# One operand of the first layer's vector instructions moved to PSUM in a two-layer graph kernel

## The chip, the cores and the metric

The kernel runs on one core of one Trainium2 chip. The metric is the device time of one execution in microseconds, the median over the runs of a kernel. Lower is better. The engines are called by the profile's names: PE (TensorE), DVE (VectorE), ACT (ScalarE), POOL (GpSimd) and SP (SyncE).

## The reference

Two message-passing layers run over 6250 nodes of 128 features and 200000 edges sorted by destination `dst`. Each layer normalises the nodes, applies a ReLU, sends messages along the edges and adds the sum per destination to the nodes. The first layer, the one that is changed, is an attention layer with 8 heads:

```python
z = (feat @ W).reshape(N, HEADS, PER_HEAD)
el = jnp.einsum('nhp,hp->nh', z, attn_l)
er = jnp.einsum('nhp,hp->nh', z, attn_r)
e = jax.nn.leaky_relu(el[src] + er[dst], negative_slope=NEG_SLOPE)
emax = jax.ops.segment_max(e, dst, num_segments=N)
a = jnp.exp(e - emax[dst])
denom = jax.ops.segment_sum(a, dst, num_segments=N)
agg = jax.ops.segment_sum(z[src] * a[:, :, None], dst, num_segments=N)
out = agg / jnp.maximum(denom, 1e-09)[:, :, None] + bias
```

The second layer gathers `h[src]` again, multiplies it with edge attributes and with the outputs of a small network over 8 edge features, and sums by `dst`. It is not changed.

## The kernel before

The edges lie in 1563 tiles of 128, one edge on each partition. Sixteen tiles make a block, so there are 98 blocks. A first stage computes a row of 136 numbers for every node (128 of `z`, 8 of `el`) and writes it to a table in HBM; `er` stays on the chip.

The first layer then works block by block, one pass of a loop over `g` for each:

- **Gathers.** `take_rows` fetches the table rows of a block's source nodes, one indirect DMA for each tile, issued by POOL at line L832 (`gather`) three blocks ahead. The index column `src_col` (the profile's `fsrc`) lies in SBUF. The destination tiles come from a pool of five. In 31 blocks one of the sixteen tiles comes row by row on SP's queue instead (L1067), so POOL issues 1516 gathers in this loop, after 16 for the first block.
- **One-hot matrices.** `one_hot` (L1086) compares a row 0 to 127 (`iota`) with the position of each edge's destination in its window. It makes four tiles per DVE instruction, four instructions per block, called through `ends_of`. PE turns them (`turned`, L1132), ACT copies them out (L1134), and PE multiplies them with `er` in three bf16 parts (`er_of`, L1143); `er_sum` (L1149) adds the parts.
- **Logits and maxima.** `logits` adds `el` and `er` (L1156), applies the leaky ReLU (L1157) and turns the result on PE into a PSUM bank `pe` (L1160). `maxima` runs two segmented scans along the edges, forward (L1166) and backward (L1168). `neighbours` moves the edge values of the maxima between tiles and blocks with four small matmuls (L1175 to L1184), and ACT copies the two columns out (L1187).
- **Weights and sums.** `weights`, one block later, joins the neighbours' maxima with the block's own (L1193, L1195), subtracts (L1198) and takes the exponential. `weighted` (L1210) scales the rows, and `sums` (L1215) adds them per destination on PE.
- **Nodes.** In every second block a tile of 128 nodes is finished (`node_x` to `node_out`): lines L1225 to L1238 on DVE, then a transpose into a PSUM bank `p_n` (L1259), a ReLU on ACT (L1261), a matmul into the same bank (L1266) and a copy out (L1268), which is written to the second layer's table.

The order of the work on PE, DVE, ACT and SP is written out by hand as the order of these calls. A semaphore wait therefore holds everything behind it on its engine. POOL has only gathers to issue. After the loop the last three groups of tiles are written out one by one. The second layer's gathers start when the last rows of its table have been written. In that layer `iota` already lies in PSUM (tile `held`, the profile's `p_i`), and so does one factor of the messages.

Of the kernel before, what the change touches and what calls it, by code (L numbers as in the profile page):

```python
# [18 lines left out]
P = 128  # L19
H = 8  # L20
# [9 lines left out]
KB = 16  # L30
# [933 lines left out]
def even_edges(tc, v):  # L964
    nc = tc.nc
    NX, TU, TG, NB, KT, MC = (v[k] for k in (
        "NX", "TU", "TG", "NB", "KT", "MC"))
    t0, t1, ident, eps, er3, z_first, dstt, nums = (v[k] for k in (
        "t0", "t1", "ident", "eps", "er3", "z_first", "dstt", "nums"))
    xp, dstc, y4, f8, bias, out, moments, deviation, normal, gather, tiles_of = (v[k] for k in (  # L970
        "xp", "dstc", "y4", "f8", "bias", "out", "moments", "deviation", "normal", "gather", "tiles_of"))
    with ExitStack() as ctx:
# [6 lines left out]
        iota = const.tile([P, P], F32, name="fiota")  # L979
# [29 lines left out]
        shift = const.tile([P, 3, P], F32, name="fshift")  # L1009
# [35 lines left out]
        with tc.tile_pool(name="fat_ps", bufs=1, space=PSUM) as at_ps:  # L1045
            col = const.tile([P, P], F32, name="fcol")
            n = NB - 1
# [35 lines left out]
        def one_hot(t, m, iota=iota):  # L1083

            s = s_pool.tile([P, 4, P], F32, name="s")
            nc.vector.tensor_tensor(s[:, :m], iota[:, None, :].to_broadcast([P, m, P]),  # L1086
                                    dloc[:, t : t + m].unsqueeze(2).to_broadcast([P, m, P]),
                                    OP.is_equal)
            return s
# [17 lines left out]
        with tc.manual_schedule(engines=in_order), \  # L1107
# [2 lines left out]
                tc.tile_pool(name="l0_ps", bufs=1, space=PSUM) as l0_ps:  # L1110


            def ends_of(c, q):

                if 4 * q < c["kt"] and q == len(c.setdefault("s", [])):
                    c["s"].append(one_hot(c["b"] * KB + c["o"] + 4 * q, min(4, c["kt"] - 4 * q)))

            def masks_of(c):
                o, kr = c["o"], c["kt"] * H
# [23 lines left out]
                        nc.tensor.matmul(c["p_er"][:, 4 * q + k].rearrange("p s h -> p (s h)"),  # L1143
                                         c["d", q][:, k, :], er_w, start=True, stop=True)

            def er_sum(c):
                kt = c["kt"]
                er = c["er"] = l0.tile([P, KB, H], F32, name="er")
                nc.vector.tensor_reduce(er[:, :kt], c["p_er"][:, :kt].rearrange("p t s h -> p t h s"),  # L1149
                                        AX.X, OP.add)  # L1150

            def logits(c, bank="pe"):
                kt = c["kt"]
                kr = kt * H
                e_s = l0.tile([P, KB, H], F32, name="e_s")
                nc.vector.tensor_add(e_s[:, :kt], c["z"][:, :kt, F:], c["er"][:, :kt])  # L1156
                nc.vector.scalar_tensor_tensor(e_s[:, :kt], e_s[:, :kt], 0.2, e_s[:, :kt],  # L1157
                                               op0=OP.mult, op1=OP.max)
                pe = c["pe"] = l0_ps.tile([P, 512], F32, name=bank, bufs=2 if bank == "pe" else 1)
                nc.tensor.transpose(pe[:kr, :P], e_s[:, :kt].rearrange("p t h -> p (t h)"), ident)  # L1160

            def maxima(c):

                kr, mk, pe = c["kt"] * H, c["mk"], c["pe"]
                mx = c["mx"] = l0.tile([P, 2, P], F32, name="mx", bufs=4)
                nc.vector.tensor_tensor_scan(mx[:kr, 0, :], mk[:kr, :P], pe[:kr, :P], 0.0,  # L1166
                                             OP.add, OP.max)
                nc.vector.tensor_tensor_scan(mx[:kr, 1, ::-1], mk[:kr, P:0:-1], mx[:kr, 0, ::-1], 0.0,  # L1168
                                             OP.add, OP.max)

            def neighbours(c, before, after):

                kr, pe, mx = c["kt"] * H, c["pe"], c["mx"]
                up, dn = pe[:kr, 2 * P : 2 * P + 1], pe[:kr, 2 * P + 1 : 2 * P + 2]
                nc.tensor.matmul(dn, shift[:kr, 2, :kr], mx[:kr, 1, P - 1 :], start=True,  # L1175
                                 stop=before is None)
                if before is not None:
                    kb = before["kt"] * H
                    nc.tensor.matmul(dn, shift_to[kb][:kb, :kr], before["mx"][:kb, 1, P - 1 :],
                                     start=False, stop=True)  # L1180
                nc.tensor.matmul(up, shift[:kr, 0, :kr], mx[:kr, 1, 0:1], start=True, stop=after is None)
                if after is not None:
                    ka = after["kt"] * H
                    nc.tensor.matmul(up, shift[:ka, 1, P - kr :], after["mx"][:ka, 1, 0:1],  # L1184
                                     start=False, stop=True)
                ud = c["ud"] = l0.tile([P, 2], F32, name="ud")
                nc.scalar.copy(ud[:kr], pe[:kr, 2 * P : 2 * P + 2])  # L1187

            def weights(c):

                kr, pe, mx, mk, ud = c["kt"] * H, c["pe"], c["mx"], c["mk"], c["ud"]
                m1 = l0.tile([P, P], F32, name="m1")
                nc.vector.scalar_tensor_tensor(m1[:kr], mk[:kr, P + 1 : 2 * P + 1], ud[:kr, 0:1],  # L1193
                                               mx[:kr, 1, :], op0=OP.add, op1=OP.max)
                nc.vector.scalar_tensor_tensor(m1[:kr], mk[:kr, 2 * P + 1 :], ud[:kr, 1:2],  # L1195
                                               m1[:kr], op0=OP.add, op1=OP.max)
                a = l0.tile([P, P], F32, name="a")
                nc.vector.tensor_sub(a[:kr], pe[:kr, :P], m1[:kr])  # L1198
                nc.scalar.activation(a[:kr], a[:kr], AF.Exp)
                nc.tensor.transpose(pe[:, P : P + kr], a[:kr], ident[:kr, :kr])  # L1200
                nc.scalar.copy(c["z"][:, : c["kt"], F:],  # L1201
                               pe[:, P : P + kr].rearrange("p (t h) -> p t h", h=H))
# [50 lines left out]

            def node_t(u):
                n = u["n"]
                p_n = l0_ps.tile([P, 512], F32, name="p_n")
                p_n = u["p_n"] = p_n.rearrange("p (j f) -> p j f", f=P)
                for j in range(n):
                    nc.tensor.transpose(p_n[:, j, :], u["xn"][:, j, :], ident)  # L1259
                h_t = u["h_t"] = l0n.tile([P, 2, P], F32, name="h_t")  # L1260
                nc.scalar.activation(h_t[:, :n], p_n[:, :n], AF.Relu)  # L1261

            def node_s(u):
                i, n, p_n = u["i"], u["n"], u["p_n"]
# [17 lines left out]
            shift_to = {}  # L1282
# [6 lines left out]
            NG = len(cs)  # L1289
# [51 lines left out]
            for g in range(NG - 3):  # L1341
                take_rows(g + 3)
                filled(0, g, cs[g]["z"], ZW)
                rows_until(rows, g + 0.5)
                for n in late:
                    node_out(n)
                if g % 2 == 0 and g // 2 + 2 < NX - 2:
                    node_rows(g // 2 + 2, 1)
                rows_until(rows, g + 1)
                c, b4 = cs[g], (cs[g - 1] if g else None)  # L1350
                n1 = cs[g + 1] if g + 1 < NG else none
                n2 = cs[g + 2] if g + 2 < NG else none
# [12 lines left out]
                turned(n1, 1)  # L1365
                er_of(n1, 0)
                if b4:
                    weights(b4)
                for n in nodes:
                    node_x(n)  # L1370
                er_of(n1, 1)
                turned(n1, 2)
                if b4:
                    bank_of(b4)
                    weighted(b4, 0)
                turned(n1, 3)
                er_of(n1, 2)
                if b4:
                    weighted(b4, 8)
                for n in nodes:  # L1380
                    node_d(n)
                    node_h(n)
                ends_of(n2, 2)
                er_of(n1, 3)
                if b4:
                    sums(b4, 0)
                for n in nodes:
                    node_t(n)
                if n1 is not none:
                    er_sum(n1)  # L1390
                ends_of(n2, 3)
                for n in nodes:
                    node_s(n)
                late = nodes
                if b4:
                    sums(b4, 8)
                if g == NG - 4:
                    for q in range(4):
                        ends_of(c1, q)
                    masks_of(c1)  # L1400
                    for q in range(4):
                        turned(c1, q)
                        er_of(c1, q)
                    er_sum(c1)
            node_rows(NX - 2, 2)
            for n in late:
                node_out(n)
# [373 lines left out]
```

## Time and profile before

| What | Value |
|---|---|
| Median of three runs | 6103.52 us (6102.03 to 6114.51) |
| Profiled execution, its own time | 3960.89 us |
| Its span, first to last instruction | 3959.1 us |
| POOL busy, share of the span | 2955.5 us, 75% |
| PE busy, share of the span | 2823.8 us, 71% |
| DVE busy, share of the span | 2189.6 us, 55% |
| ACT busy, share of the span | 1390.4 us, 35% |

The profile is of one execution, and its own time lies 2142.6 us under the median of the runs. Times inside it add up to its own span, not to the median. In the profile the first layer's loop takes the stretch from about 70 to 2000 us, the second layer that from about 2030 us to the end. In a row of the costliest groups the two numbers after the first bar are busy microseconds and mean nanoseconds of one instruction; after the second bar stands the idle time of the engine just before them and what ended it. "Issue" means that nothing the profile shows was waited for.

### The profile page before, as it was taken

How to read it: one execution, taken by the hardware profiler on the slowest of the kernel's cores; microseconds unless marked ns; L12 is line 12 of the kernel's file. 1: busy time of each engine (PE TensorE's matmuls, PEld its weight loads, DVE VectorE, ACT ScalarE, POOL GpSimd, SP SyncE). 2: the span in 40 equal slices, each digit the busy share in tenths (PEclk: the TensorE clock that was granted, in tenths of full speed). 3: DMA queues.
4: the chain of work that ended last, by engine and by line, in shares of the span. 5: the costliest groups of instructions: out<-in, count | busy, mean ns of one | idle time of the engine just before them, and what ended most of it. 6: DMA issues, size and time to landing. Idle time of an engine off the chain costs nothing. (4 is left out here: it accounts for less than half of the span.)

```text
span 3959.1 us, 62173 instructions
## 1 busy us (share of the span) xinstructions
PE 2823.8 (71%) x14593; PEld 2368.9 (60%) x14593; DVE 2189.6 (55%) x5379; ACT 1390.4 (35%) x3512; POOL 2955.5 (75%) x3096
## 2 busy tenths in 40 slices
PE   3666666666666666666676888788788787788777
PEld 3655555555665666565555666566566566666565
DVE  5444444444444444444455776666666666666666
ACT  3322222223222323222233444444444444344443
POOL 6777777777777777777757777777777777777776
PEclk6666666666666666666678999999999999999999
DMA  6222222222222222222212222222222222222221
GB/s 176 58 60 61 60 61 61 60 59 61 60 61 59 59 61 60 61 59 60 59 45 60 62 62 62 62 63 62 61 63 62 61 61 61 62 61 62 61 62 49
DMA packets 188124, 249.35 MB, mean 63 GB/s; under 512 B 77888, under 2 KB 137952, under 8 KB 187744
## 3 DMA queue, kind: packets, MB, share of 16 engines
q0 software_dynamic: 98048, 207.27, 22.2%
q1 hardware_dynamic: 89408, 37.92, 3.7%
q8 instruction: 118, 1.93, 0.2%
q14 instruction: 262, 2.15, 0.2%
q10 hardware_dynamic: 288, 0.07, 0.0%
HBM read 234.73 MB, written 9.99 MB: 62 GB/s over the span
## 5 line engine op out<-in xcount | busy, mean ns | idle before, releaser
L832 POOL DMA_INDIRECT g<-ft,fsrc x3048 | 2921.8, 959 | 957.7 <-issue 873.5
L1544 PE MATMUL p_u<-mj,s 128*128 128x256 f32 x3126 | 794.3, 398 | 263.7 <-DVE mj L1536 261.9
L1544 PEld LDWEIGHTS p_u<-mj,s 128*128 128x128 f32 x3126 | 585.5, 195 | 442.0 <-DVE mj L1536 369.3
L1215 PE MATMUL p_u<-g,s 128*128 128x136 f32 x3062 | 578.9, 368 | 0.5 <-DVE g L1210 0.5
L1215 PEld LDWEIGHTS p_u<-g,s 128*128 128x128 f32 x3062 | 554.2, 272 | 0.6 <-DVE g L1210 0.6
L1511 ACT ACTIVATE p_w<-p_w,yb 128x64 f32<-128x64 f32 x1563 | 450.3, 288 | 119.5 <-PE p_w L1507 79.6
L1527 DVE TENSOR_TENSOR vy<-g,p_i 128x384 f32<-128x384 f32 x391 | 215.6, 551 | 462.4 <-DMA g<-ft,fsrc 374.6
L1156 DVE TENSOR_TENSOR e_s<-g,er 128x128 f32<-128x128 f32 (+1 forms) x98 | 28.4, 290 | 735.0 <-DMA g<-ft,fsrc 697.0
L1507 PE MATMUL p_w<-fa3p,h 128*128 128x256 f32 x1564 | 409.7, 385 | 0.0
L1132 PE MATMUL p_d<-fident,s 128*128 128x128 f32 x1563 | 390.5, 416 | 5.2 <-DVE s L1086 5.2
L1507 PEld LDWEIGHTS p_w<-fa3p,h 128*128 128x128 f32 x1564 | 288.7, 195 | 118.7 <-issue 52.1
L1160 PE MATMUL pe<-fident,e_s 128*128 128x128 f32 x98 | 39.8, 406 | 444.6 <-DVE e_s L1157 444.6
L1125 ACT COPY mk<-p_m 128x385 f32<-128x385 f32 (+1 forms) x99 | 47.7, 481 | 875.1 <-PE p_m L1122 875.1
L1132 PEld LDWEIGHTS p_d<-fident,s 128*128 128x128 f32 x1563 | 316.9, 228 | 44.2 <-DVE s L1086 32.1
L1492 ACT ACTIVATE h<-p_h,fb 128x512 f32<-128x512 f32 x196 | 134.7, 687 | 568.8 <-PE p_h L1490 567.5
L1134 ACT CAST d<-p_d 128x512 bf16<-128x512 f32 x391 | 228.9, 586 | 198.5 <-PE p_d L1132 149.9
L1210 DVE TENSOR_TENSOR g<-g,pe 128x1024 f32<-128x1024 f32 x193 | 225.4, 1209 | 127.3 <-ACT g L1201 121.8
L1160 PEld LDWEIGHTS pe<-fident,e_s 128*128 128x128 f32 x98 | 16.7, 170 | 461.2 <-issue 452.5
L1086 DVE TENSOR_TENSOR s<-p_i,fdloc 128x512 f32<-128x512 f32 x391 | 266.0, 680 | 14.5 <-ACT p_i L1486 14.5
L1086 DVE TENSOR_TENSOR s<-fiota,fdloc 128x512 f32<-128x512 f32 x391 | 265.8, 681 | 5.9 <-ACT fmasks L1036 5.8
L1490 PE MATMUL p_h<-ft,fa1p 128*128 128x128 f32 x1568 | 217.7, 284 | 62.5 <-DMA ft<-in_e_f_dram 62.4
L1490 PEld LDWEIGHTS p_h<-ft,fa1p 128*128 128x128 f32 x1568 | 214.2, 200 | 79.3 <-issue 63.7
(177 smaller groups left out, 3363.2 us busy)
## 6 DMA issues: line engine op xcount, KB each, us to landing
r<-ft SPq DMA_DIRECT2D x3968, 0.5 KB
r<-ft SPq DMA_DIRECT2D x3968, 0.5 KB
g<-ft,fsrc POOLq DMA_INDIRECT x3048
ft<-in_e_f_dram SPq DMA_DIRECT2D x98, 64.0 KB
yb<-in_e_y_dram SPq DMA_DIRECT2D x98, 32.0 KB
fx_all<-in_e_xp_dram SPq DMA_DIRECT2D x48, 64.0 KB
ft<-sv SPq DMA_DIRECT2D x47, 64.0 KB
out_dram<-fx_all SPq DMA_DIRECT2D x47, 64.0 KB
```

What stands on the lines that cost most here:

```text
L832: nc.gpsimd.indirect_dma_start(out=to[:, k, :width], out_offset=None, in_=table, in_offset=bass.IndirectOffsetOnAxis(ap=src_col[:, t : t + ...
L1086: nc.vector.tensor_tensor(s[:, :m], iota[:, None, :].to_broadcast([P, m, P]), dloc[:, t : t + m].unsqueeze(2).to_broadcast([P, m, P]), OP. ...
L1132: nc.tensor.transpose(p_d[:, k, :], c["s"][q][:, k, :], ident)
L1134: nc.scalar.copy(d[:, :m], p_d[:, :m])
L1210: nc.vector.tensor_mul(zh, zh, p_a[:, k0 : k0 + m].unsqueeze(3).to_broadcast([P, m, H, D]))
L1215: nc.tensor.matmul(c["p_u"][:, :ZW], c["s"][k // 4][:, k % 4, :], c["z"][:, k, :], start=c["o"] + k == 0, stop=c["o"] + k == KT[c["b"]] - 1)
L1490: nc.tensor.matmul(p_h[:, q, :], a1p[:, q0 + q, :], c["ft"], start=True, stop=True)
L1492: nc.scalar.activation(c["h1"], p_h, AF.Silu, bias=b1)
L1507: nc.tensor.matmul(w[:, k : k + n].rearrange("p k a u -> p (k a u)"), c["h2"][q // 4][:, q % 4, :], a3p[:, :n].rearrange("p k f -> p (k f) ...
L1511: nc.scalar.activation(w[:, k, ::2, :], w[:, k, ::2, :], AF.Copy, scale=c["yb"][:, k0 + k, 0:1])
L1527: nc.vector.tensor_mul(vy, v_n, y_p)
L1544: nc.tensor.matmul(blk[b]["p_u"][:, :MW], u["s"][:, k, :], u["mj"][:, k, :], start=k0 + k == 0, stop=k0 + k == KT[b] - 1)
```

## The change

`iota`, `er`, both scans' results and the joined maxima are put into PSUM. A bank `p_n`, until now taken anew for each tile of nodes, becomes one permanent tile that holds the node work, `er` (columns 128 to 255) and `iota` (columns 384 to 511). The scans write into free columns of the block's own bank `pe`. [...]ACT copies the first and last column of the backward scan to a small SBUF tile `mx`. Two calls of `er_sum` at the end of the loop keep an SBUF tile (`aside`).

```diff
+            p_n = l0_ps.tile([P, 512], F32, name="p_n")
+            er_p, iota_p = p_n[:, P : 2 * P].rearrange("p (t h) -> p t h", h=H), p_n[:, 3 * P :]
+            nc.scalar.copy(iota_p, iota)
...
-                    c["s"].append(one_hot(c["b"] * KB + c["o"] + 4 * q, min(4, c["kt"] - 4 * q)))
+                    c["s"].append(one_hot(c["b"] * KB + c["o"] + 4 * q, min(4, c["kt"] - 4 * q), iota_p))
...
-            def er_sum(c):
+            def er_sum(c, aside=False):
-                er = c["er"] = l0.tile([P, KB, H], F32, name="er")
+                er = c["er"] = l0.tile([P, KB, H], F32, name="er") if aside else er_p
...
+                pe = c["pe"] = p_n if bank == "p_n" else l0_ps.tile([P, 512], F32, name=bank, bufs=2)
...
-                mx = c["mx"] = l0.tile([P, 2, P], F32, name="mx", bufs=4)
-                nc.vector.tensor_tensor_scan(mx[:kr, 0, :], mk[:kr, :P], pe[:kr, :P], 0.0,
+                m0, m1 = pe[:kr, P : 2 * P], pe[:kr, 3 * P :]
+                nc.vector.tensor_tensor_scan(m0, mk[:kr, :P], pe[:kr, :P], 0.0, OP.add, OP.max)
+                nc.vector.tensor_tensor_scan(m1[:, ::-1], mk[:kr, P:0:-1], m0[:, ::-1], 0.0,
                                              OP.add, OP.max)
-                nc.vector.tensor_tensor_scan(mx[:kr, 1, ::-1], mk[:kr, P:0:-1], mx[:kr, 0, ::-1], 0.0,
-                                             OP.add, OP.max)
+                mx = c["mx"] = l0.tile([P, 2], F32, name="mx", bufs=4)
+                nc.scalar.copy(mx[:kr], m1[:, :: P - 1])
...
-                nc.vector.scalar_tensor_tensor(m1[:kr], mk[:kr, P + 1 : 2 * P + 1], ud[:kr, 0:1],
-                                               mx[:kr, 1, :], op0=OP.add, op1=OP.max)
-                nc.vector.scalar_tensor_tensor(m1[:kr], mk[:kr, 2 * P + 1 :], ud[:kr, 1:2],
-                                               m1[:kr], op0=OP.add, op1=OP.max)
+                m1, m2 = pe[:kr, 3 * P :], pe[:kr, P : 2 * P]
+                nc.vector.scalar_tensor_tensor(m2, mk[:kr, P + 1 : 2 * P + 1], ud[:kr, 0:1],
+                                               m1, op0=OP.add, op1=OP.max)
                 a = l0.tile([P, P], F32, name="a")
-                nc.vector.tensor_sub(a[:kr], pe[:kr, :P], m1[:kr])
+                nc.vector.scalar_tensor_tensor(a[:kr], mk[:kr, 2 * P + 1 :], ud[:kr, 1:2],
+                                               m2, op0=OP.add, op1=OP.max)
+                nc.vector.tensor_sub(a[:kr], pe[:kr, :P], a[:kr])
...
             def node_t(u):
-                p_n = l0_ps.tile([P, 512], F32, name="p_n")
-                p_n = u["p_n"] = p_n.rearrange("p (j f) -> p j f", f=P)
+                u["p_n"] = p_n.rearrange("p (j f) -> p j f", f=P)
...
-                    er_sum(n1)
+                    er_sum(n1, g == NG - 4)
...
-                    er_sum(c1)
+                    er_sum(c1, True)
```

More of the change, by code (lines that the diff above doesn't have):

```diff
@@ L1158, in logits @@
                                                op0=OP.mult, op1=OP.max)
-                pe = c["pe"] = l0_ps.tile([P, 512], F32, name=bank, bufs=2 if bank == "pe" else 1)
                 nc.tensor.transpose(pe[:kr, :P], e_s[:, :kt].rearrange("p t h -> p (t h)"), ident)
@@ L1174, in neighbours @@
                 up, dn = pe[:kr, 2 * P : 2 * P + 1], pe[:kr, 2 * P + 1 : 2 * P + 2]
-                nc.tensor.matmul(dn, shift[:kr, 2, :kr], mx[:kr, 1, P - 1 :], start=True,
-                                 stop=before is None)
+                nc.tensor.matmul(dn, shift[:kr, 2, :kr], mx[:kr, 1:], start=True, stop=before is None)
                 if before is not None:
                     kb = before["kt"] * H
-                    nc.tensor.matmul(dn, shift_to[kb][:kb, :kr], before["mx"][:kb, 1, P - 1 :],
+                    nc.tensor.matmul(dn, shift_to[kb][:kb, :kr], before["mx"][:kb, 1:],
                                      start=False, stop=True)
-                nc.tensor.matmul(up, shift[:kr, 0, :kr], mx[:kr, 1, 0:1], start=True, stop=after is None)
+                nc.tensor.matmul(up, shift[:kr, 0, :kr], mx[:kr, 0:1], start=True, stop=after is None)
                 if after is not None:
                     ka = after["kt"] * H
-                    nc.tensor.matmul(up, shift[:ka, 1, P - kr :], after["mx"][:ka, 1, 0:1],
+                    nc.tensor.matmul(up, shift[:ka, 1, P - kr :], after["mx"][:ka, 0:1],
                                      start=False, stop=True)
@@ L1189, in weights @@
             def weights(c):
-                kr, pe, mx, mk, ud = c["kt"] * H, c["pe"], c["mx"], c["mk"], c["ud"]
-                m1 = l0.tile([P, P], F32, name="m1")
-                nc.vector.scalar_tensor_tensor(m1[:kr], mk[:kr, P + 1 : 2 * P + 1], ud[:kr, 0:1],
-                                               mx[:kr, 1, :], op0=OP.add, op1=OP.max)
-                nc.vector.scalar_tensor_tensor(m1[:kr], mk[:kr, 2 * P + 1 :], ud[:kr, 1:2],
-                                               m1[:kr], op0=OP.add, op1=OP.max)
+                kr, pe, mk, ud = c["kt"] * H, c["pe"], c["mk"], c["ud"]
+                m1, m2 = pe[:kr, 3 * P :], pe[:kr, P : 2 * P]
+                nc.vector.scalar_tensor_tensor(m2, mk[:kr, P + 1 : 2 * P + 1], ud[:kr, 0:1],
+                                               m1, op0=OP.add, op1=OP.max)
                 a = l0.tile([P, P], F32, name="a")
-                nc.vector.tensor_sub(a[:kr], pe[:kr, :P], m1[:kr])
+                nc.vector.scalar_tensor_tensor(a[:kr], mk[:kr, 2 * P + 1 :], ud[:kr, 1:2],
+                                               m2, op0=OP.add, op1=OP.max)
+                nc.vector.tensor_sub(a[:kr], pe[:kr, :P], a[:kr])
                 nc.scalar.activation(a[:kr], a[:kr], AF.Exp)
@@ L1255, in node_t @@
                 n = u["n"]
-                p_n = l0_ps.tile([P, 512], F32, name="p_n")
-                p_n = u["p_n"] = p_n.rearrange("p (j f) -> p j f", f=P)
+                u["p_n"] = p_n.rearrange("p (j f) -> p j f", f=P)
                 for j in range(n):
-                    nc.tensor.transpose(p_n[:, j, :], u["xn"][:, j, :], ident)
+                    nc.tensor.transpose(u["p_n"][:, j, :], u["xn"][:, j, :], ident)
                 h_t = u["h_t"] = l0n.tile([P, 2, P], F32, name="h_t")
-                nc.scalar.activation(h_t[:, :n], p_n[:, :n], AF.Relu)
+                nc.scalar.activation(h_t[:, :n], u["p_n"][:, :n], AF.Relu)
             def node_s(u):
```

## The prediction

> **What bounds the kernel now.** I read the page's costliest groups first.
>
> ```profile
> L832 POOL DMA_INDIRECT g<-ft,fsrc x3048 | 2921.8, 959 | 957.7 <-issue 873.5
> L1156 DVE TENSOR_TENSOR e_s<-g,er 128x128 f32<-128x128 f32 (+1 forms) x98 | 28.4, 290 | 735.0 <-DMA g<-ft,fsrc 697.0
> ```
>
> POOL's gathers are busy 2921.8 us, and of the 957.7 us idle before them 873.5 wait for nothing that the profile shows. Together that is 3879.5 us of the 3959.1 us span: POOL issues gathers without a pause. DVE, at the head of each first-layer block (L1156), waited 697 us for gathered rows. So in both layers the pace is POOL's cost per gather, and PE, DVE and ACT have slack.
>
> Next the same line by stage (columns: stretch, its length, POOL busy and count, PE clock, DMA share, GB/s), and its shortest/median/longest duration in ns.
>
> ```profile
> 500.00:1000.00 500.00, 380.41 (x393) 0.66 0.27 60
> 1000.00:1500.00 500.00, 380.49 (x393) 0.65 0.27 60
> ...
> 2500.00:3000.00 500.00, 377.82 (x401) 0.97 0.24 62
> 3000.00:3500.00 500.00, 377.86 (x401) 0.98 0.24 62
> ```
>
> ```profile
> L832 POOL DMA_INDIRECT g<-ft,fsrc x393: 940/944/1360, 999.8 to 1499.9; - x197
> ```
>
> ```profile
> L832 POOL DMA_INDIRECT g<-ft,fsrc x401: 940/944/961, 3000.1 to 3499.6; - x134
> ```
>
> A gather takes a median of 944 ns in both layers. In the first layer some take up to 1360, in the second none over 961. The period from one gather to the next is 500/393 = 1272 ns against 500/401 = 1247.
>
> The timeline of one block shows which are long (columns: start, duration in us, engine, line):
>
> ```profile
> 1010.61 0.68 DVE L1086 TENSOR_TENSOR s<-fiota,fdloc 128x512 f32<-128x512 f32 x1
> ...
> 1011.02 1.09 POOL L832 DMA_INDIRECT g<-ft,fsrc  x1 [0.30 <-issue]
> ...
> 1011.77 0.42 DVE L1168 TENSOR_TENSOR_SCAN mx<-mk,mx 128x128 f32<-128x128 f32 x1
> ...
> 1012.12 0.67 DVE L1086 TENSOR_TENSOR s<-fiota,fdloc 128x512 f32<-128x512 f32 x1
> ...
> 1012.41 1.18 POOL L832 DMA_INDIRECT g<-ft,fsrc  x1 [0.30 <-issue]
> ...
> 1013.90 0.94 POOL L832 DMA_INDIRECT g<-ft,fsrc  x1 [0.30 <-issue]
> ```
>
> The gathers that start while L1086 runs take 1.09 and 1.18 us; the one at 1013.90, with no such instruction beside its start, takes 0.94. L1086 ends 0.27 and 0.38 us after those starts, the stretches are 0.15 and 0.24: both fit a read some 0.13 us into the gather that waits until DVE has finished. In the second layer the same compare, `iota` in PSUM, runs as often and stretches nothing.
>
> **What the Trainium skill says.** *SBUF — State Buffer*, section "Who interferes with whom": a DVE instruction with two SBUF inputs contends with a GpSimd instruction that reads SBUF, since its second input comes through the interface that the two share. The trace agrees (1.09 and 1.18 us against 0.94). The same section infers that `tensor_tensor` does not stall descriptor generation, as that only writes; for these gathers, whose index lies in SBUF, the trace decides otherwise. *PSUM — Partial Sum Buffer*, rule after "PSUM bank collisions raise a hardware error": engines are to be kept apart by bank, not by address. I therefore count on waits between DVE, PE and ACT over the shared bank `p_n`; the trace of before can't show them. *VectorE: DVE Perf Modes*, in its errata section, gives DVE a larger fixed term for PSUM than for SBUF sources, 120 against 58 cycles. The trace doesn't show that here: the compare takes 681 ns from SBUF (L1086 with `fiota`) and 680 with PSUM (`p_i`).
>
> **The change part by part.**
>
> *Stretching of the gathers, removed.* From 100 to 2000 us the windows give 1492 gathers busy 1446.2 us, a mean of 969; from 2100 us on 1478 busy 1392.6, a mean of 942. The difference, 27 ns, times the loop's 1516 gathers is 41 us. From the periods it is (1272 - 1247) x 1516 = 38. I take 40 as all that is to be had here, on the path throughout.
>
> *What still has two SBUF inputs.* L1157 (98 x 0.29 us), L1225, L1237 and L1238 (48 each, 0.28 to 0.29). If they fell anywhere in the 1.25 us period, the expected delay of one is 0.29^2 / (2 x 1.25) = 0.034 us; times 98 + 144 = 8 us. They hold little in the trace, where the DVE order is tied to the landing of a gather and so to POOL's phase; but the phase can shift. Between 0 and 8, I take 3. Gain left: 37 us.
>
> *Durations on DVE.* Four compares of 0.68, the scans of 0.42, L1193 and L1195 of 0.35, L1156 of 0.29 and the sum L1149 of 0.55 us stay, one operand or the output in PSUM. From the compare's 681 against 680 I take no change. The bound is +-64 ns (62 cycles, the page's figure as an estimate) on some ten instructions: 0.6 us per block either way, hidden by DVE's 697/90 = 7.7 us wait per block, and worth 63 us over 98 blocks if that cover were gone.
>
> *ACT's new copies.* `iota` once, 0.27 us (L1567, the same copy), while the first gathers run. `mx`, 98 copies of 2 columns; the nearest row, L1187, takes 0.16 us: 15.7 us on an engine 35% busy. On ACT the copy sits between the casts L1134, and the cast behind it waits for the backward scan; the last neighbour matmul (L1184) now waits for the copy. In the block shown that scan ends at 1012.19 and the cast starts at 1012.55, so little is held: 0.3 us per block, hidden by the same 7.7 us. No DMA is added or moved, and SP's queue and POOL's keep their order.
>
> *Waits over bank `p_n`.* In every second block L1149 (`er_sum`) is ordered after the node transpose L1259 and ReLU L1261. In the block shown it started at 1021.41 and L1261 ended at 1023.44, so it starts some 2.0 us later. The last compare of the block, queued behind it on DVE, goes with it, and so does the matmul L1266, which comes after that compare by bank: from 1023.48 to about 1023.44 + 0.55 + 0.68 = 1024.7, 1.2 us later. Behind L1266 on PE wait the last 8 matmuls of `sums`, 2.0 us, which then end near 1027. The next rows land at 1029.03: hidden, with 2 us to spare, and a late block doesn't stop POOL, which issues three blocks ahead into five tiles. From zero (no such waits) to 2.0 us x 48 = 96 us if nothing covered them; I take zero.
>
> *The end of the layer*, where nothing covers:
>
> ```profile
> 2003.98 0.23 DVE L1156 TENSOR_TENSOR e_s<-g,er 128x64 f32<-128x64 f32 x1 [2.46 <-DMA g<-ft,fsrc]
> ...
> 2029.89 0.94 POOL L832 DMA_INDIRECT g<-ft,fsrc  x1 [28.32 <-DMA ft<-sv]
> ```
>
> POOL stands still for 28.32 us, and the work between these lines is a chain. It gets one `mx` copy and its hand-over (0.3 us) and perhaps a wait over the bank: 0 to 2 us, I take 1.
>
> *Sum*: -40 + 3 + 1 = -36 us on the profiled execution's own 3960.89 (span 3959.1, 1.8 around it): 3925.
>
> **From the profiled time to the median.** The median of the runs, 6103.52, is 2142.6 us (54%) above that time, and the profile does not show where they spend it. I carry the difference over in microseconds: 6103.5 - 36 = **6067**. If all of it scaled, it would be 36 x 1.54 = 55: 6048.
>
> **The rivals.**
>
> 1. *More of the contention in the timed runs.* If every DVE instruction that loses its second SBUF input held POOL for its whole length, the change would free 266 (L1086) + 41 (L1168) + 68 (L1193, L1195) + 28 (L1156) = 403 us: 5700. For it: something makes the timed runs longer. Against it: in the profile 40 of the 403 are lost, and most gathers beside these instructions have the median length.
> 2. *Another bound, or no effect.* If the timed runs are paced by something that the change doesn't touch (SP's single rows, a PE at a lower clock, time outside the loop's pace), or if the stretch has another cause than the operand, nothing moves: 6103.
> 3. *Slower: the shared bank.* If in the timed runs the chain of DVE, PE and ACT paces a block rather than POOL, the waits over `p_n` count: 48 x 1.2 to 2.0 us is 58 to 96, plus 98 x 0.3 for the `mx` hand-over, 29. The middle, 77 + 29, gives 6210. It decides once a block's slack, 7.7 us in the profile, falls under about 2 us. Against it stand DVE's 697 us of waiting for rows; for it, only that 2142.6 us are unexplained.
>
> **How the numbers follow.** A measurement of this kernel can tell about 0.2% from no change, 12 us. I give the forecast 0.52 (its own range 6040 to 6090), rival 1 0.13 (5700 to 6040), rival 2 0.16, rival 3 0.19 (6116 to 6260). Faster: 0.52 + 0.13 = 0.65; same 0.16; slower 0.19. The range 5990 to 6150 leaves out some 0.08 of rival 1 below and 0.11 of rival 3 above.
>
> **What the profile after would show.** Right: the mean of L832 in the first layer near 944 ns and none far above 960, some 399 gathers per 500 us, L1086 still near 680 ns, the standstill before the second layer near 28 to 30 us, a span near 3923. The bank's waits would stand before L1149 and L1266 in every second block, with DVE's wait at L1156 still several us per block. Wrong: gathers that stay at 969 although the operand moved (another cause); L1156 no longer waiting for rows (rival 3); or the gain in the profile with none in the median (rival 2).

## The result, and the profile after

The changed kernel takes 6203.03 us (median of 6 runs, 6197.33 to 6211.51), the kernel before beside it 6102.77 (6093.23 to 6115.85). The ratio is 1.0162, 95% interval [1.0147, 1.0178]: 1.6% slower, where 6067 was forecast.

The same program runs at two paces, by series of runs (each on one chip): the kernel before takes 3954 to 3961 us in some series (the profile shown of it is of this short pace) and 6103 or 6191 in others (the long pace, the "slow pace" of the expectations), so differences of times are taken within one series unless the text says otherwise. The profile after is of the long pace, span 6199.2 us, own time 6201.12, so it can't be set against the profile of before line by line. Its counterpart at the short pace is the run `e2_after` below. The kernel before was never traced at the long pace.

The page of the changed kernel, first POOL's busy tenths in 40 slices, then three rows of the costliest groups:

```profile
POOL 6354454544445444454534444444444444444442
...
L832 POOL DMA_INDIRECT g<-ft,fsrc x3048 | 2885.4, 947 | 3174.9 <-issue 1510.7
...
L1140 ACT CAST d<-p_d 128x512 bf16<-128x512 f32 x391 | 228.1, 587 | 881.3 <-remote 746.2
...
L1155 DVE TENSOR_REDUCE p_n<-p_er 128x128 f32<-128x384 f32 (+1 forms) x97 | 54.7, 563 | 663.6 <-remote 257.3
```

The gathers themselves are as expected: 947 ns in the mean, hardly any stretch left (the longest of the first layer takes 1047). But POOL is no longer the bound: its idle time has grown from 957.7 to 3174.9 us, and in both layers its gathers fill about half of the time or less. Before the casts behind PE's transposes ACT stands idle for 881.3 us in all, most of it put down to something that the profile can't name ("remote"), and before `er_sum` (L1155, L1149 in the kernel before) DVE waits 663.6.

L832 by stage (stretch, length, POOL busy and count, PE clock, DMA share, GB/s), and its shortest/median/longest duration between 1000 and 1500 us:

```profile
500.00:1000.00 500.00, 252.35 (x267) 0.63 0.18 41
1000.00:1500.00 500.00, 239.77 (x255) 0.62 0.17 39
2500.00:3000.00 500.00, 222.71 (x236) 0.62 0.17 37
3000.00:3500.00 500.00, 238.30 (x252) 0.71 0.15 38
```

```profile
L832 POOL DMA_INDIRECT g<-ft,fsrc x255: 942/947/963, 999.4 to 1499.9; - x128
```

There are 255 to 267 gathers in 500 us where the profile before had 393. The second layer, which the change doesn't touch, has 236 to 252 where it had 401. So more than half of the distance from 3960 to 6200 us is not of the first layer and not of this change. The traces also speak against a slower PE, which rival 2 named: between 1000 and 1500 us PE is busy for 204 us at a clock of 0.62, where `e2_after` has 328 at 0.65; in the second layer (4000 to 5000 us) for 55% at 0.76, where `e2_after` (2500 to 3000) has 79% at 0.98.

A piece of the timeline shows what the long pace looks like (start, duration, engine, line; in brackets the idle time ahead and its releaser):

```profile
985.12 1.60 PE L1138 MATMUL p_d<-fident,s 128*128 128x128 f32 x8
...
994.13 0.59 ACT L1140 CAST d<-p_d 128x512 bf16<-128x512 f32 x1 [8.65 <-remote]
...
1001.13 0.59 ACT L1140 CAST d<-p_d 128x512 bf16<-128x512 f32 x1 [6.42 <-remote]
...
1006.12 0.28 ACT L1266 ACTIVATE h_t<-p_n 128x128 f32<-128x128 f32 x1 [1.87 <-PE p_n L1264]
1006.43 0.57 DVE L1155 TENSOR_REDUCE p_n<-p_er 128x128 f32<-128x384 f32 x1 [2.11 <-ACT h_t L1266]
1007.04 0.69 DVE L1086 TENSOR_TENSOR s<-p_n,fdloc 128x512 f32<-128x512 f32 x1
...
1007.87 0.46 PE L1271 MATMUL p_n<-fwup,h_t 128*128 128x128 f32 x2 [1.79 <-DVE s L1086]
...
1010.96 0.95 POOL L832 DMA_INDIRECT g<-ft,fsrc  x1 [10.64 <-issue]
```

PE finished the transposes at about 986.7, but ACT's cast of them started at 994.13, and the next one 7.0 us after it. All this time POOL issued gathers, one per 1.25 us. From about 1000.3 POOL paused; then the hand-overs between engines were short (the compare L1086 ends at 1007.73, the node matmul L1271 behind it starts at 1007.87), until POOL resumed at 1010.96. So at the long pace gathers and the other engines' work partly alternate.

This stretch is no exception. Of the casts between 100 and 2950 us, 282 were ready (PE done, ACT free) while POOL gathered: 130 of them started more than 1 us later, up to 20.5. Of the 100 that were ready in POOL's pauses, 7 started more than 1 us later, 2.5 at most. In `e2_after`, with POOL gathering all the time, none of 383 did. In the stretch shown stands also the order over bank `p_n` that the prediction's rival 3 described: `er_sum` behind the ReLU L1266, the compare L1086 behind it, the node matmul L1271 behind that.

From the start of its first gather to that of its last, and counting a gather as running until the next one's start, 1.26 us at most, the first layer's loop took 2897 us, with POOL running for 1896 and pausing for 1001. The second layer took 3116 us, with 1200 of pauses. In `e2_after` the first took 1896 us with 4 of pauses, the second 1912 with none.

### The profile page after: what moved, and what is told of

It reads as the page before. It is cut to its first block, busy times and chain, and to the rows that moved or that the text cites. A ratio compares the mean times of both kernels' runs of the same rounds, so it can differ in the third digit from the quotient of the medians.

```text
span 6199.2 us, 62249 instructions
## 1 busy us (share of the span) xinstructions
PE 2970.3 (48%) x14593; PEld 2462.3 (40%) x14593; DVE 2207.9 (36%) x5379; ACT 1390.7 (22%) x3612; POOL 2919.2 (47%) x3096
## 5 line engine op out<-in xcount | busy, mean ns | idle before, releaser
L832 POOL DMA_INDIRECT g<-ft,fsrc x3048 | 2885.4, 947 | 3174.9 <-issue 1510.7
L1549 PE MATMUL p_u<-mj,s 128*128 128x256 f32 x3126 | 925.2, 448 | 719.5 <-DVE mj L1541 601.3
L1549 PEld LDWEIGHTS p_u<-mj,s 128*128 128x128 f32 x3126 | 679.9, 225 | 905.1 <-DVE mj L1541 656.2
L1534 DVE TENSOR_TENSOR p_w<-g,p_w 128x128 f32<-128x128 f32 x391 | 114.7, 293 | 1278.6 <-ACT p_w L1516 1099.6
L1149 PEld LDWEIGHTS <-d 128*128 128x128 bf16 x1563 | 99.2, 113 | 845.1 <-ACT d L1140 512.0
L1140 ACT CAST d<-p_d 128x512 bf16<-128x512 f32 x391 | 228.1, 587 | 881.3 <-remote 746.2
L1502 ACT ACTIVATE h<-p_h,fb 128x512 f32<-128x512 f32 x196 | 134.9, 688 | 1167.9 <-remote 841.8
L1560 PE MATMUL p_n<-fwout,m_t 128*128 128x128 f32 x192 | 57.1, 451 | 561.6 <-ACT m_t L1558 561.6
L1138 PE MATMUL p_d<-fident,s 128*128 128x128 f32 x1563 | 320.1, 357 | 5.2 <-issue 5.2
L1499 PE MATMUL p_h<-h,fa2p 128*128 128x512 f32 x392 | 245.9, 714 | 125.2 <-ACT h L1497 98.7
L1497 ACT ACTIVATE h<-p_h,fb 128x512 f32<-128x512 f32 x196 | 134.6, 687 | 698.2 <-PE p_h L1495 391.4
L1155 DVE TENSOR_REDUCE p_n<-p_er 128x128 f32<-128x384 f32 (+1 forms) x97 | 54.7, 563 | 663.6 <-remote 257.3
L1149 PE MATMUL p_er<-fer,d 128*128 128x24 bf16 x784 | 55.3, 185 | 467.7 <-ACT d L1140 285.2
L1086 DVE TENSOR_TENSOR s<-p_i,fdloc 128x512 f32<-128x512 f32 x391 | 269.0, 688 | 14.0 <-ACT h L1497 14.0
L1138 PEld LDWEIGHTS p_d<-fident,s 128*128 128x128 f32 x1563 | 258.2, 192 | 39.3 <-issue 30.6
```

Of the source, the lines that this page charges most:

```text
L832: nc.gpsimd.indirect_dma_start(out=to[:, k, :width], out_offset=None, in_=table, in_offset=bass.IndirectOffsetOnAxis(ap=src_col[:, t : t + ...
L1138: nc.tensor.transpose(p_d[:, k, :], c["s"][q][:, k, :], ident)
L1140: nc.scalar.copy(d[:, :m], p_d[:, :m])
L1499: nc.tensor.matmul(p_h.rearrange("p q e -> p (q e)"), a2p, c["h1"].rearrange("p q e -> p (q e)"), start=True, stop=True)
L1549: nc.tensor.matmul(blk[b]["p_u"][:, :MW], u["s"][:, k, :], u["mj"][:, k, :], start=k0 + k == 0, stop=k0 + k == KT[b] - 1)
```

## The experiments

**The kernel before again, and the single rows of SP.** One block in three gets 128 of its rows from single DMAs that SP issues (L1067). Without them POOL gathers all rows.

```diff
-        by_row = [b for b in range(3, NB - 2) if b % 3 == 0]
+        by_row = []
```

> The kernel before, unchanged, for a trace that belongs to the timed runs. All theories: 6100 us, not the 3961 of the first profile. Theory A (SP's single rows and POOL's gathers slow each other): in its trace SP issues about one row in 0.75 us on the mean, in spells of 0.7 us per instruction while POOL gathers. Theory B (something in every block apart from the rows): rows at the 0.32 us pace in most stretches, and long waits elsewhere.

Measured: 3960.51 us, ratio 1.0 [0.9991, 1.0008] to the runs of the kernel before beside it (3960.68). These runs had the short pace, where 6100 had been expected.

> The kernel before with all tiles gathered by POOL, none row by row on SP (62 gathers more, 7936 row transfers fewer). Theory A: POOL paces again, 3126 gathers at 1.25 to 1.27 us and some 110 us around them, 4020 to 4080 us. Theory B: 6100 us plus 60 to 130 for the gathers added.

Measured: 4022.02 us, ratio 1.0154 [1.0137, 1.0171]. There are 3110 gathers in place of 3048; 62 x 1.25 us is 77, and 61 more came.

> The changed kernel with all tiles gathered by POOL. Theory A: 3990 to 4040 us, and 30 to 45 below the kernel before without rows, since only then the stretch of the gathers counts. Waits over the shared bank as the cause of the 100 us: still slower than the kernel before without rows, by up to 100. Theory B: 6200 us plus 60 to 130.

Measured: 4000.92 us, ratio 1.0104 [1.0087, 1.0121], 21 us less than the kernel before without the rows, where 30 to 45 were expected. Without the rows there was less stretch to remove: L832 has a mean of 954 ns in `e1_before_norows`, 957 in `e1_before` and 945 here. At the short pace SP's rows are no bound. At the long pace these two kernels did not run, so this part of rival 2 is not decided there.

**Iota alone.** The kernel before with `iota` in a permanent bank `p_n` beside the node work; scans, maxima and `er` stay in SBUF.

```diff
+            p_n = l0_ps.tile([P, 512], F32, name="p_n")
+            iota_p = p_n[:, 3 * P :]
+            nc.scalar.copy(iota_p, iota)
...
-                    c["s"].append(one_hot(c["b"] * KB + c["o"] + 4 * q, min(4, c["kt"] - 4 * q)))
+                    c["s"].append(one_hot(c["b"] * KB + c["o"] + 4 * q, min(4, c["kt"] - 4 * q), iota_p))
```

> Of the change only iota in the permanent bank p_n (and the node work in it); er, the scans and the joined maxima stay in SBUF, no mx copy. Waits over the bank: half of the 100 us or more, 6150 to 6200. The copies and waits of the maxima as the cause: 6100. More instruction-by-instruction crawling of SP because POOL gets through its gathers sooner: 6150 to 6200, as the compares cause most of the stretch.

Measured: 3926.5 us, ratio 0.9913 [0.9897, 0.993], 34 us less. The longest gather between 1000 and 1500 us takes 1062 ns, where `e1_before` has 1478. So the compare's second SBUF operand caused most of the stretch.

**The whole change and the maxima alone, at the short pace.** The second kernel has only the scans and joined maxima in PSUM, with the `mx` copies.

> The changed kernel again, unchanged. If the kernel before runs at 3960 us beside it, as in the runs just seen: the prediction's sum gives 36 less, 3925; that the change itself adds 100 us whatever the pace would give 4060. If the kernel before runs at 6100 beside it: 6200, as at first, and the cause lies in the pace of those executions.

Measured: 3916.77 us beside 3960.51, ratio 0.9888 [0.9872, 0.9905]: 43.7 us less. Of its profile, the page's rows, the first layer's stage and L832's durations:

```profile
L832 POOL DMA_INDIRECT g<-ft,fsrc x3048 | 2880.4, 945 | 958.1 <-issue 866.1
...
L1163 DVE TENSOR_TENSOR e_s<-g,p_n 128x128 f32<-128x128 f32 x96 | 27.5, 287 | 579.1 <-DMA g<-ft,fsrc 563.7
```

```profile
500.00:1000.00 500.00, 377.78 (x401) 0.65 0.28 61
```

```profile
L832 POOL DMA_INDIRECT g<-ft,fsrc x401: 940/944/1054, 1000.0 to 1499.5; - x134
```

POOL is the bound, 401 gathers in 500 us as in the second layer, none over 1054 ns where 1360 stood. DVE still waits 563.7 us for rows at the head of a block (L1163; 697.0 at L1156 before). Of the 133 us less, some 41 are the shorter loop (1896 us in place of 1937), so the block's work grew by some 92 and remained hidden. DVE's wait at L1155 behind the ReLU is 91.2 us in this trace: the order over bank `p_n` costs its time at the short pace too, but out of that cover.

> Of the change only the scans and the joined maxima in the bank pe and the mx copies; iota, er and p_n as before. At 3960 us for the kernel before: iota alone gave -34, so what is left of 36 is 0 to 5, 3955 to 3961. At 6100 for the kernel before: 6200 if the copies and waits of the maxima are what makes the changed kernel slower, 6100 if it is the bank p_n.

Measured: 3960.02 us, ratio 0.9999 [0.999, 1.0008]: no effect by itself at the short pace.

**Serial gathers.** To see what the change costs when gathers don't hide the block's work, the first layer's gathers are issued only at the end of the block before, into a ring of two tiles.

```diff
-            for g in range(1, 3):
-                take_rows(g)
+            take_rows(1)
...
             for g in range(NG - 3):
-                take_rows(g + 3)
...
                 if b4:
                     sums(b4, 8)
+                if g:
+                    take_rows(g + 1)
```

> The kernel before, with one thing changed in the first layer: the gathers of a block are issued only when the block before it is finished (two destination tiles in place of five), so that POOL's gathers and the block's work on DVE, PE and ACT follow each other and do not overlap. It imitates on any chip the alternation of the slow trace. Both theories: some 88 blocks x (19.4 us period - 7.7 us wait for rows, about 11.7 us of block work) = 1030 us more than before, so near 5000 us where the kernel before takes 3960, and gathers of 944 ns with no stretched ones, as DVE is idle beside them.

Measured: 5668.17 us beside 3953.53 for the kernel before, 1715 more and not 1030: a block's work that the gathers don't cover takes 1723/98 = 17.6 us here (POOL's pauses in the first layer add up to 1723 us). The last rows' landing and the way back to POOL are part of it, which the estimate from DVE's wait left out. The purpose, gathers with nothing beside them, was met: DVE was busy 22 us beside gathers and 878 in pauses.

> The changed kernel with the same serial gathers. Theory (the waits over bank p_n and the hand-over of mx count in full once the gathers do not hide the block's work): 60 to 130 us longer than the serial kernel before, 100 the likeliest. Rival A (these waits are small or absorbed within the block even so, and the loss at the slow pace comes from something else in those executions): within 30 us of the serial kernel before. Rival B (the stretch of gathers would be saved here too): shorter by about 40 us.

Measured: 5772.96 us (5766.31 to 5782.61), 104.8 more than the serial kernel before (5665.92 to 5671.43). The theory's likeliest value was 100.

> Serial gathers, and of the change only iota in bank p_n beside the node work (scans, joined maxima and er stay in SBUF, no mx copy). It has the ordering of L1266 behind the compares and of the compares behind the node work, without that of er_sum and without the mx hand-over. Theory: it carries the larger part of the loss over the bank, 40 to 80 us over the serial kernel before; the rest of the serial changed kernel's loss is the mx hand-over (29 us estimated) and er. Rival A: within 20 us of the serial kernel before.

Measured: 5720.35 us, 52.2 over the serial kernel before: half of the loss.

> Serial gathers, the whole change, but the node work (transposes L1264, matmuls L1271) takes a bank of p_d's ring of two in place of p_n, so that only DVE uses p_n in the loop: all the added waits over bank p_n are gone, the mx hand-over stays. Theory: the loss of the serial changed kernel falls to the mx hand-over, 10 to 40 us over the serial kernel before. Rival A: no different from the serial changed kernel.

```diff
             def node_t(u):
-                u["p_n"] = p_n.rearrange("p (j f) -> p j f", f=P)
+                u["p_n"] = l0_ps.tile([P, 4, P], F32, name="p_d", bufs=2)
```

Measured: 5656.59 us (5656.1 to 5658.27), 11.6 *less* than the serial kernel before, outside the 10 to 40 more that were expected. With only DVE in bank `p_n`, the whole loss is gone although the `mx` copies are still there.

The groups show the waits. `er_sum` in the serial kernel before, then `er_sum` and the node matmul in the serial changed kernel, then `er_sum` with the node work apart:

```profile
L1149 DVE TENSOR_REDUCE er<-p_er 128x128 f32<-128x384 f32 (+1 forms) x99 | 54.0, 546 | 18.8 <-PE p_er L1143 18.8
```

```profile
L1155 DVE TENSOR_REDUCE p_n<-p_er 128x128 f32<-128x384 f32 (+1 forms) x97 | 54.7, 563 | 113.7 <-ACT h_t L1266 96.7 <-PE p_er L1149 12.1
...
L1271 PE MATMUL p_n<-fwup,h_t 128*128 128x128 f32 x100 | 31.3, 409 | 83.3 <-DVE s L1086 82.1 <-ACT h_t L1266 1.2
```

```profile
L1155 DVE TENSOR_REDUCE p_n<-p_er 128x128 f32<-128x384 f32 (+1 forms) x97 | 54.6, 563 | 21.8 <-PE p_er L1149 12.1
```

96.7 us behind the ReLU is new in the second and gone in the third. The same place in the timeline, serial kernel before and serial changed kernel:

```profile
1409.93 0.55 DVE L1149 TENSOR_REDUCE er<-p_er 128x128 f32<-128x384 f32 x1
...
1411.81 0.28 ACT L1261 ACTIVATE h_t<-p_n 128x128 f32<-128x128 f32 x1 [1.87 <-PE p_n L1259]
...
1412.14 0.49 PE L1266 MATMUL p_n<-fwup,h_t 128*128 128x128 f32 x2 [0.37 <-ACT h_t L1261]
...
1412.47 2.02 PE L1215 MATMUL p_u<-g,s 128*128 128x136 f32 x16
```

```profile
1527.14 0.28 ACT L1266 ACTIVATE h_t<-p_n 128x128 f32<-128x128 f32 x1 [1.88 <-PE p_n L1264]
1527.45 0.57 DVE L1155 TENSOR_REDUCE p_n<-p_er 128x128 f32<-128x384 f32 x1 [2.12 <-ACT h_t L1266]
1528.05 0.69 DVE L1086 TENSOR_TENSOR s<-p_n,fdloc 128x512 f32<-128x512 f32 x1
...
1528.88 0.77 PE L1271 MATMUL p_n<-fwup,h_t 128*128 128x128 f32 x2 [1.78 <-DVE s L1086]
...
1529.44 3.83 PE L1221 MATMUL p_u<-g,s 128*128 128x136 f32 x16
```

From the ReLU's start to the last matmuls of `sums` it is 0.66 us before and 2.30 after, and after that gap PE also runs these sixteen matmuls more slowly, 3.83 us against 2.02; why is not shown. In the mean of the loop's node tiles the first is 0.71 against 2.19 us, the second 2.04 against 2.88, and from the ReLU's start to POOL's next gather it is 3.53 against 5.85: 2.32 x 48 node tiles = 111 us, about the whole loss. With `iota` alone in the bank that way takes 4.73 us (1.20 x 48 = 58), with the node work apart 3.54.

**The node work apart, gathers as before.** The candidate for a kernel that keeps the gain and drops the waits.

> The changed kernel with the node work (L1264, L1266, L1271, L1273) in a bank of p_d's ring of two in place of p_n, gathers as in the kernel before. Where the kernel before takes 3960 us: like the changed kernel, 3917 (within 8), since the waits over p_n are hidden there by the gathers and the stretch is gone in both. Were the kernel before beside it at its slow pace (6100), theory: the 100 us of loss are gone, 6030 to 6110; rival A (the loss at that pace is not from the bank): 6180 to 6220 like the changed kernel.

> The changed kernel itself, beside the same runs of the kernel before. Where that takes 3960 us: 3917 (within 5), 1.1% shorter. Where it takes 6100: 6203, 1.6% longer.

Measured, short pace (kernel before 3960.98): 3922.98 us, 0.9904 [0.9886, 0.9922], and for the changed kernel 3923.23, 0.9905 [0.9888, 0.9923]. No difference between them, as expected where the waits are hidden. They show in what covers them: DVE waits 667.6 us for rows at L1163 with the node work apart and 568.1 in the changed kernel.

**One series at the long pace** (kernel before 6190.68).

> The changed kernel with the node work in a bank of p_d's ring. Where the kernel before beside it takes 3960: 0.99 of it, as seen already. Where it takes 6100: 0.985 to 1.001 of it by the theory, 1.013 to 1.018 if the loss of 100 us there has another cause than bank p_n.

Measured: 6255.49 us (6251.66 to 6264.72), ratio 1.0106 [1.0078, 1.0135], 65 us *more* than the kernel before. That is outside what the theory expected (0.985 to 1.001) and under what the other cause expected (1.013 to 1.018). The whole change has 1.0162 in its own series. So bank `p_n` may account for about a third of the loss at this pace (0.0056 of 0.0162), and some 65 us have another cause. The third is not shown: the kernels before of the two series lie 88 us apart, and the second layer, which is the same program, took 3139 us in `e5_apart` and 3116 in the changed kernel.

> Serial gathers and the whole change, but er stays in SBUF, so that er_sum (L1155) is not ordered behind the ReLU L1266 over bank p_n; the compare behind it still is. If er in the bank is the other half of the loss: like the serial kernel with iota alone, 40 to 65 us over the serial kernel before (5668), where the serial changed kernel has 105. If the other half is the mx hand-over: 90 to 110 over it.

Measured: 7041.37 us (7035.34 to 7054.44). The expected figures were for the short pace and can't be compared as they stand.

> Serial gathers, and of the change only the scans and joined maxima in PSUM with the mx copies; iota and er stay in SBUF, the node work has p_n alone. If the hand-over of mx costs 0.3 us per block on the exposed chain, as rival 3 priced it: 29 us over the serial kernel before. As the serial kernel with the node work apart came out 12 us shorter than that one: -15 to +5.

Measured: 6996.92 us (6990.31 to 7002.93). There is no serial kernel before in this series, so the maxima are not sized against it. The pair tells one thing: `iota` in bank `p_n` costs 44.5 us here over the kernel without it, near the 52.2 of the short pace. And where little overlaps, the long pace costs little: the first layer took 3647 us in `e5_serial_maxima`, and 3616 in the serial kernel before at the short pace (across two series). The second layer, where POOL gathers beside the others, took 3153 against 1912. Of the casts in `e5_serial_maxima` between 100 and 3700 us, 380 of 382 were ready in POOL's pauses and started within 0.1 us; the two that were ready beside a gather started 20 us later.

**The rest.** Two last attempts to divide the 65 us: `iota` in a bank that only DVE uses, and the maxima alone beside the kernel before.

> The kernel before with iota in PSUM in a bank that only DVE uses (the node work takes a bank of p_d's ring); scans, joined maxima and er stay in SBUF, no mx copy. Where the kernel before takes 3960: 0.991, as with iota in bank p_n. Where it takes 6100 to 6200: 0.998 to 1.002 if the 65 us left with the node work apart come from the mx copies and the maxima in PSUM; 1.008 to 1.014 if they come from iota in PSUM, that is, from gathers that are no longer held by DVE.

Measured: 3919.52 us beside 3957.93, ratio 0.9902 [0.9885, 0.9919].

> The kernel before with the scans and joined maxima in PSUM and the mx copies alone, gathers as before. Where the kernel before takes 3960: 1.000 of it, as seen. Where it takes 6100 to 6200: 1.008 to 1.014 if the 65 us come from the mx copies and their hand-over; 0.998 to 1.002 if they come from iota in PSUM and the gathers that DVE no longer holds.

> The kernel before itself. Where it takes 3960: the profile as known. Where it takes 6100 to 6200: POOL pauses some 940 to 980 us in the first layer (the changed kernel 1001 to 1031), and L832 has a mean of 955 to 970 ns there if DVE still holds it; near 945 if it is hardly held, because DVE works mostly in POOL's pauses.

Measured: 3959.64, ratio 1.0 [0.9991, 1.0009], and 3959.01, ratio 0.9999 [0.999, 1.0009]. All three met the short pace, so they say nothing on the 65 us, and `e7_before` gave no trace of the long pace. They do say that at the short pace the gain is `iota`'s nearly alone.

## Why the prediction was wrong

**The step that failed** is "From the profiled time to the median": the timed runs were 54% longer than the profiled execution, the prediction said that the profile does not show where they spend it, and then carried the 36 us over as if the same engine were the bound there. In the one long execution of the changed kernel that was traced it is not: POOL pauses for 1001 us of the first layer's 2897, so shorter gathers buy little. "I take zero" for the waits also lost the cover that it named, DVE's 7.7 us per block. At the head of a block DVE waited over 2 us in 33 of 99 cases, where the profile before has 94, and more for the tile that SP brings (L1081) than for gathered ones:

```profile
L1163 DVE TENSOR_TENSOR e_s<-g,p_n 128x128 f32<-128x128 f32 x96 | 27.2, 284 | 433.2 <-ACT g L1081 221.9 <-DMA g<-ft,fsrc 173.1 <-ACT sv L1273 38.1
```

*Stretching of the gathers, -40.* Right in mechanism and size at the short pace: -43.7 and -37.8 us for the whole change in two series, -34.2 for `iota` in bank `p_n`. What the page *SBUF — State Buffer* of the Trainium skill says in "Who interferes with whom" on DVE instructions with two SBUF inputs agrees with these gathers beside the compare; its inference that `tensor_tensor` doesn't stall descriptor generation does not (at most 1360 ns before, 1054 after). At the long pace the changed kernel has no such stretch either (1047 ns at most in the first layer), and no gain.

*What still has two SBUF inputs, +3; the end of the layer, +1.* The longest gather of 1054 ns shows that a little of the first remains. POOL's standstill at the end of the layer, from gather start to gather start, was 29.8 and 28.5 us in two runs of the changed kernel at the short pace, 29.3 before: nothing to be seen. The sum of -36 lay within 8 us of both measurements.

*Durations on DVE, 0.* Right: in `e2_after` the first layer's compare takes 682 ns where it took 681, `er_sum` 563 where 544.

*The `mx` hand-over, 29 us where nothing covers it.* Mis-sized: with serial gathers, the copies in place and the node work apart, the kernel was 11.6 us shorter, not 29 longer. In the traces at the short pace the neighbour matmul L1184 starts 1.09 us after the backward scan's end, in the mean. After the change the copy starts 0.63 us after it, takes 0.17, and the matmul (L1190) follows 0.26 later: 1.06. PE had other work in that time. With serial gathers it is 1.43 us before and with the node work apart alike. What the copies do at the long pace is open.

*Waits over bank `p_n`, 0 of a possible 96.* The wait that the upper bound priced came as priced: 96.7 us at L1155 with the gathers out of the way, 2.1 us each. They follow the rule of the page *PSUM — Partial Sum Buffer* (after "PSUM bank collisions raise a hardware error") to guard PSUM by bank and not by address: `er` and the node work lie in different columns of `p_n`. What it cost without cover is another sum: of the 111 us worked out above, 71 (1.48 x 48) are the later start of the last matmuls, and 40 (0.84 x 48) their slower pace, which the prediction left out. Taking zero was right at the short pace, where the change gains as forecast, and wrong without cover.

*Rival 3, 6210.* It came within 7 us of 6203, but the agreement is partly chance. Its mechanism is shown for serial gathers (104.8 us, gone when the node work leaves the bank). At the long pace itself, removing it left 65 of the about 100 us. Its second term, the 29 us, did not show where it could be seen, with serial gathers.

**What stays open.** First, the 65 us: they come with the maxima in PSUM and the `mx` copies, with gathers that DVE no longer holds, or with the node work in the ring of `p_d`; no kernel with one of these alone was measured at the long pace, and without a trace of the kernel before at that pace it is not shown in which part of the program the loss lies. Second, what the long pace is. It may belong to the chip: six series on four chips had the short pace, `e5` on a fifth the long one, and the chip of the first series is not on record. The waits of ACT in the first layer of the changed kernel (total us, times, longest) give two leads:

```profile
ACT d L1140 <- remote: 677.6, 121, 13.2
...
ACT g L1081 <- issue: 219.4, 15, 26.5
ACT g L1081 <- DMA r<-ft: 190.4, 15, 26.9
```

One lead is the hand-overs that come late beside gathers. SP issued its rows in POOL's pauses too, so the rows alone do not make them late. The other is these single rows: L1081 copies them, and ACT waited 410 us before it in 30 cases, 190 of them put down to the rows. While POOL gathered, a row followed the last one after 0.71 us in the median, in its pauses after 0.32, as in `e2_after` beside gathers. SP was at work nearly all the time (its instructions started over 2 us apart for only 308 of 2860 us), so the rows may be a bound of the long pace, as rival 2 allowed. With the node work apart the same wait is larger:

```profile
ACT g L1081 <- DMA r<-ft: 413.1, 18, 35.8
...
ACT g L1081 <- issue: 129.6, 12, 16.0
```

These are readings of traces; no run without the rows was made at the long pace. No version was found that is faster than the kernel before at both paces: the kernels with the node work or `iota` apart gain 1% at the short one, the first of them loses 1.1% at the long one, and the second was not measured there.

## What to carry to other kernels

When the profiled execution is much shorter than the timed runs, the bound read from it may not be theirs: a gain counted on one engine then needs its own chance, and every wait costed at nothing "because it is hidden" should be priced without its cover. An operand in a PSUM bank that other engines also use ordered those engines after each other here; a bank that one engine alone uses avoids it (with the node work in the ring of `p_d` the serial kernel was 116 us shorter, and at the short pace it cost nothing).

## What was not expected of the hardware

- One program with the same data had two paces by series, 3960 and 6103 to 6191 us; the traces place the difference in stretches where POOL issues gathers beside other engines. In the long one, 130 of 282 casts that were ready beside gathers started more than 1 us late, up to 20.5, and SP's rows came 0.71 us apart; in POOL's pauses 7 of 100 casts were late, by 2.5 us at most, and the rows came 0.32 us apart.
- With gathers and block work one after the other, the first layer took nearly the same at both paces, 3616 and 3647 us (two kernels that differ in the maxima alone).
